# A batch's second-layer results kept in one PSUM bank, and added to x1 and the bias once per batch

## The chip, the cores and the metric

The kernel runs on one core of a Trainium2 chip. A time is the device time of one execution in microseconds (us). A core has five engines that each work through their own instructions strictly in order: TensorE (PE, with its weight loads PEld), VectorE (DVE), ScalarE (ACT), GpSimd (POOL) and SyncE (SP, which here only issues DMAs). They wait for each other by semaphores.

## What is computed

Input are 16 batches of 1024 nodes with 64 channels, `x`, and their adjacency matrices `adj` of zeros and ones. Two graph layers follow each other, each with a residual and a layer norm:

```python
x = _layernorm(x + _L0_gnn_ref(x, adj, nodemask, W1, b1, W2, b2))   # neighbours thinned out, weighted
                                                                    # quantiles of the rest, a small MLP
# second layer, h = x:
messages = jnp.einsum('bij,bjh->bih', adjacency, h)
node_in = jnp.concatenate([h, messages], axis=-1)
dh = jnp.tanh(node_in @ W1 + b1) @ W2 + b2
x = _layernorm(x + dh)
```

The change is in the second layer, at `... @ W2 + b2` and `x + dh`.

## The kernel before, in words

The batches are handled in groups (`GROUPS`, 2, 4, 4, 4 and 2 batches). Each group goes through three kinds of work, and those of different groups run beside each other.

- `prepare` (`list_batch`, L612, and `weigh_group`, L731) thins out the neighbours of each node and sorts the nodes by degree into lists in HBM.
- Chunks of tiles of 128 nodes: `fill` brings the neighbours' rows into slots (`slots_a`), by indirect DMAs on POOL (L846) or, in `ChunkByPE`, by one-hot matmuls on PE (`hot`, L982, and `p_slots`, L990). `select` (L862) sorts the slots with minima and maxima on DVE (L875), weights the chosen ones on ACT (`terms`, L897), sums them on PE (`p_g`, L894 and L899) and runs the MLP of the first layer: `p_h` (L903), `h_t` (L905), `p_y` (L908). DVE adds the bias (L910), the mask and the residual and does the layer norm (L550 to L558), and POOL scatters the rows to x1 in HBM (L916).
- `messages` (L1014) is the second layer of one batch. It loads the batch's x1 (`x_n` in the profile, L1018). For each of the batch's eight tiles (NT = 8, QT = 1) it then loads 128 rows of `adj` (L1024), transposes them on PE (`p_adj`, L1029) and copies them with ACT (`adj_t`, L1030), transposes x1's tile (`p_x`, L1035) and multiplies the adjacency with x1 (`p_msg`, L1039). ACT copies both into `node_t` (L1036, L1041). Then come the two layers of the MLP, `p_z` (L1043), `z_t` with tanh on ACT (L1045) and `p_d` (L1048). DVE adds the bias while it reads `p_d` from PSUM (L1049). After the eighth tile, DVE adds x1 (L1051) and does the layer norm, and SP stores the batch (L1053).

PSUM has eight banks. The pools give out the buffers of a tag in turn, in the order in which the code asks for them, and an instruction that writes a buffer waits until the last reader of its earlier use is done. The tags are "tr" and "ta" (one bank each), "rv" (three), "m" (two) and "y" (one). Tag "m" serves `p_g`, `p_h`, `p_x`, `p_msg`, `p_z` and two matmuls of `list_batch`. Tag "y" serves `p_y` and `p_d`.

The order of the work is set twice. The loop at the end (L1097 to L1141) calls the generators of the chunks (`fill`, `select`), of `prepare` for the next group and of `finish_group` (which calls `messages`) for the last group in turn, in shares. Then the scheduler of the tile framework places the instructions of all of them on the engines by its own estimate of when each will be ready. So the instructions of a `messages` tile stand between the sorting steps of a chunk on DVE, and between other matmuls on PE. Whatever stands behind a waiting instruction on the same engine waits too. After the last chunk only the `messages` of the last group are left. The code after L1158 is for other inputs; with these it does not run.

Of the kernel before, what the change touches and what calls it, by code (L numbers as in the profile page):

```python
# [9 lines left out]
F32 = mybir.dt.float32  # L10
# [10 lines left out]
P = 128  # L21
# [395 lines left out]
def kernel(  # L417
# [15 lines left out]
    nc = tc.nc  # L433
    B, N, C = x.shape
    H = w1a.shape[1]
    NT = N // P
    HALF = N // 2
    HT = NT // 2
    XCOL = N + 2 * INFO
    ROW = XCOL + 2 * C  # L440
    QT = 1
# [79 lines left out]
    def row_of(v, n, name):  # L521
        t = const.tile([P, n], F32, name=name)
        nc.sync.dma_start(t, bass.AP(tensor=v.tensor, offset=v.offset, ap=[[0, P], [1, n]]))
        return t
# [6 lines left out]
    def matrix_of(v, name):  # L531
        t = const.tile(list(v.shape), F32, name=name)
        nc.sync.dma_start(t, v)
        return t

    w1a_s, w2a_s = matrix_of(w1a, "w1a_s"), matrix_of(w2a, "w2a_s")
    w1b_s, w2b_s = matrix_of(w1b, "w1b_s"), matrix_of(w2b, "w2b_s")
    b1a_c, b1b_c = column_of(b1a, H, "b1a_c"), column_of(b1b, C, "b1b_c")
    b2a_r, b2b_r = row_of(b2a, C, "b2a_r"), row_of(b2b, C, "b2b_r")

    def bcast(v, n):
        return v[:, :, None].to_broadcast([v.shape[0], v.shape[1], n])
# [47 lines left out]
    ps_m = sort.enter_context(tc.tile_pool(name="ps_m", bufs=2, space=PSUM))  # L590
# [195 lines left out]
    class Chunk:  # L786
# [75 lines left out]
        def select(self):  # L862
            g, n, f = self.g, self.n, self.n * C
            bufs = (self.a.rearrange("p k t c -> p k (t c)"), self.b)
            x_s = self.x_s

            def view(buf, at, steps):
                v = bufs[buf][:, at]
                return bass.AP(tensor=v.tensor, offset=v.offset,
                               ap=[v.ap[0]] + [[s * f, c] for c, s in steps] + [[1, f]])  # L870

            for i, (op, rb, ra, side, ab, aa, bb, ba, dims) in enumerate(self.net["steps"]):
                if i % 4 == 3:
                    yield
                nc.vector.tensor_tensor(  # L875
                    view(rb, ra, [(d[0], d[1 + side]) for d in dims]),
                    view(ab, aa, [(d[0], d[1]) for d in dims]),
                    view(bb, ba, [(d[0], d[2]) for d in dims]),
                    op=ALU.min if op == "min" else ALU.max)
            yield  # L880
            y = work.tile([P, TMAX, C], F32, name="y")[:, :n]
            for h in range(0, n, HT):
                e = min(n, h + HT)
                cols = (e - h) * P
                g_t = work.tile([C, HALF], F32, name="g_t", tag="gh", bufs=1)
                p = ps_m.tile([P, 512], F32, name="p_g", tag="m")
                places = len(self.net["places"])
                for t2 in range(h, e, 2):
                    for first in range(0, places, 4):
                        count = min(4, places - first)  # L890
                        for t in range(t2, min(t2 + 2, e)):
                            col = slice((t - h) * P, (t - h + 1) * P)
                            if first == 0:
                                nc.tensor.matmul(p[:C, col], x_s[:, t], ident, start=t == h, stop=False)  # L894
                            terms = work.tile([P, 4, C], F32, name="terms")
                            for i, v in enumerate(self.chosen(t, first, count)):
                                nc.scalar.mul(terms[:, i], v,  # L897
                                              g.weight(self.t0 + t, first + i))
                                nc.tensor.matmul(p[:C, col], terms[:, i], ident, start=False,  # L899
                                                 stop=t == e - 1 and first + i == places - 1)  # L900
                nc.scalar.copy(g_t[:, :cols], p[:C, :cols])
                p = ps_m.tile([P, 512], F32, name="p_h", tag="m")
                nc.tensor.matmul(p[:H, :cols], w1a_s, g_t[:, :cols], start=True, stop=True)  # L903
                h_t = work.tile([H, HALF], F32, name="h_t", tag="gh", bufs=1)
                nc.scalar.activation(h_t[:, :cols], p[:H, :cols], AF.Relu, bias=b1a_c)  # L905
                p_y = ps_m.tile([P, HT, C], F32, name="p_y", tag="y", bufs=1)
                for t in range(h, e):
                    nc.tensor.matmul(p_y[:, t - h, :], h_t[:, (t - h) * P:(t - h + 1) * P], w2a_s,  # L908
                                     start=True, stop=True)
                nc.vector.tensor_add(y[:, h:e], p_y[:, :e - h],  # L910
                                     b2a_r[:, None, :].to_broadcast([P, e - h, C]))
            nc.vector.tensor_mul(y, y, bcast(g.mask[:, self.t0:self.t0 + n], C))
            nc.vector.tensor_add(y, y, x_s)
            layer_norm(work, y, y)
            for t in range(n):
                nc.gpsimd.indirect_dma_start(  # L916
                    out=g.x1, out_offset=bass.IndirectOffsetOnAxis(
                        ap=g.local[:, self.t0 + t:self.t0 + t + 1], axis=0),
                    in_=y[:, t, :], in_offset=None)
            yield  # L920
# [93 lines left out]
    def messages(g, b):  # L1014

        x1 = work.tile([P, NT, C], F32, name="x1_n", bufs=1)
        n0 = (b - g.b0) * N
        nc.sync.dma_start(x1, g.x1[n0:n0 + N, :].rearrange("(t p) c -> p t c", p=P))  # L1018
        d = work.tile([P, NT, C], F32, name="d", bufs=1)
        for h in range(NT // QT):  # L1020
            adj_t = nets.tile([P, NT, QUART], F32, name="adj_t", bufs=1)
            for t in range(QT):
                a = rows.tile([P, N], F32, name="a", bufs=3)
                nc.sync.dma_start(a, adj[b, (h * QT + t) * P:(h * QT + t + 1) * P, :])  # L1024
                for q in range(2):
                    p = ps_t.tile([P, HT, P], F32, name="p_adj", tag="ta")
                    for j in range(HT):
                        col = (q * HT + j) * P
                        nc.tensor.transpose(p[:, j, :], a[:, col:col + P], ident)  # L1029
                    nc.scalar.copy(adj_t[:, q * HT:(q + 1) * HT, t * P:(t + 1) * P], p)  # L1030
                yield
            node_t = work.tile([2 * C, QUART], F32, name="node_t", bufs=1)
            p = ps_m.tile([P, 512], F32, name="p_x", tag="m")
            for t in range(QT):
                nc.tensor.transpose(p[:C, t * P:(t + 1) * P], x1[:, h * QT + t, :], ident)  # L1035
            nc.scalar.copy(node_t[:C], p[:C, :QUART])  # L1036
            p = ps_m.tile([P, 512], F32, name="p_msg", tag="m")
            for j in range(NT):
                nc.tensor.matmul(p[C:2 * C, :QUART], x1[:, j, :], adj_t[:, j, :],  # L1039
                                 start=(j == 0), stop=(j == NT - 1))  # L1040
            nc.scalar.copy(node_t[C:], p[C:2 * C, :QUART])  # L1041
            p = ps_m.tile([P, 512], F32, name="p_z", tag="m")
            nc.tensor.matmul(p[:C, :QUART], w1b_s, node_t, start=True, stop=True)  # L1043
            z_t = work.tile([C, QUART], F32, name="z_t", bufs=1)
            nc.scalar.activation(z_t, p[:C, :QUART], AF.Tanh, bias=b1b_c)  # L1045
            p_d = ps_m.tile([P, QT, C], F32, name="p_d", tag="y", bufs=1)
            for t in range(QT):
                nc.tensor.matmul(p_d[:, t, :], z_t[:, t * P:(t + 1) * P], w2b_s, start=True, stop=True)  # L1048
            nc.vector.tensor_add(d[:, h * QT:(h + 1) * QT], p_d, b2b_r[:, None, :].to_broadcast([P, QT, C]))  # L1049
            yield  # L1050
        nc.vector.tensor_add(d, d, x1)  # L1051
        layer_norm(work, d, d)
        nc.sync.dma_start(out[b].rearrange("(t p) c -> p t c", p=P), d)  # L1053
        yield
# [6 lines left out]
    def finish_group(g):  # L1061
        for b in range(g.b0, g.b0 + g.count):
            yield from messages(g, b)
# [100 lines left out]
    ps_m = ctx.enter_context(tc.tile_pool(name="ps_m_g", bufs=2, space=PSUM))  # L1164
# [93 lines left out]
    with tc.tile_pool(name="dense", bufs=1) as dense, tc.If(general > 0), tc.For_i(0, B, 1) as b:  # L1258
# [18 lines left out]
        with tc.For_i(0, C, 1) as c:  # L1277
# [21 lines left out]
            for t in range(NT):  # L1299
                for h in range(2):  # L1300
# [3 lines left out]
                    for k in range(NT):  # L1304
                        nc.tensor.matmul(p[:, :HALF], val_t[:, k, t * P:(t + 1) * P],
                                         before[:, k, js].rearrange("p q j -> p (q j)"),
                                         start=(k == 0), stop=(k == NT - 1))
# [43 lines left out]
```

## Time and profile before

| what | value |
|---|---|
| median of six runs | 3864.01 us (3841.45 to 3886.79) |
| the profiled execution, its own time | 3870.59 us |
| its span, first to last instruction | 3868.9 us |
| mean granted TensorE clock | 0.804 |
| L1049, DVE, add of `p_d` and bias, x128 | 28.2 us busy, 220 ns each |
| L1051, DVE, add of x1, 128x512, x16 | 10.9 us busy, 682 ns each |
| L910, DVE, add of `p_y` and bias, x51 | 16.3 us busy, 320 ns each |
| L1048, PE, `p_d` | 128 matmuls in fp32, each shown as two rows |

In a line of a group, the columns are: line of the code, engine, operation, what it writes and reads, shapes, count; then busy time in us and the mean of one in ns; then the idle time of the engine just before these instructions, and what ended most of it. In a line of waits: who waited for whom, us in total, how often, the longest. In a timeline: start in us, duration, engine, line, operation, tiles, shapes, count, and in brackets the idle time before it with what ended it. "remote" is a semaphore whose giver the profile does not show, "issue" an idle time at whose end no semaphore is seen.

### The profile page before, as it was taken

The page shows a single profiled execution, that of the slowest core. Times are in us where ns is not written, and L with a number is a line of the kernel's source. Part 1 is how long each engine was busy: PE and PEld are TensorE (multiplying, and loading weights), DVE is VectorE, ACT ScalarE, POOL GpSimd, SP SyncE. Part 2 cuts the span into 40 slices and gives each one's busy share as a digit, 9 for nine tenths or more (in the row PEclk, how much of TensorE's full clock was granted, in tenths as well). Part 3 has the DMA queues.
Part 4 walks back from the last instruction along what each step waited for, and adds up shares of the span by engine and source line. Part 5 has one row for each costly group of instructions (what it writes and reads, how often), then busy time and mean ns, then how long its engine had stood idle before and what let it go on. Part 6 is the DMA issues. An engine that isn't in the chain of part 4 may idle for free. (4 is left out here: it accounts for less than half of the span.)

```text
span 3868.9 us, 65767 instructions
## 1 busy us (share of the span) xinstructions
PE 2587.8 (67%) x24920; PEld 1971.0 (51%) x25076; DVE 2392.8 (62%) x5580; ACT 1581.0 (41%) x4045; POOL 1489.1 (38%) x1512
## 2 busy tenths in 40 slices
PE   5545776465766587656877497646778376676687
PEld 2424554244654365535765375535567264565565
DVE  4546783564767477746877376746698376775461
ACT  6423456332443244533554254423355133343353
POOL 2253261443425523652453513552422543513310
PEclk8766888687877798778988698868789687788898
DMA  3401224131312222131333122212221121121222
GB/s 121 128 19 57 80 58 132 45 104 36 85 48 79 57 76 64 41 101 42 93 85 99 40 75 72 75 32 64 71 82 47 39 76 55 38 69 48 55 69 77
DMA packets 221333, 264.34 MB, mean 68 GB/s; under 512 B 147443, under 2 KB 148050, under 8 KB 221008
## 3 DMA queue, kind: packets, MB, share of 16 engines
q1 hardware_dynamic: 174288, 189.31, 17.1%
q0 software_dynamic: 46720, 70.74, 7.0%
q8 instruction: 199, 3.26, 0.4%
q14 instruction: 126, 1.03, 0.1%
HBM read 218.20 MB, written 46.40 MB: 68 GB/s over the span
## 5 line engine op out<-in xcount | busy, mean ns | idle before, releaser
L846 POOL DMA_INDIRECT slots_a<-in_x_dram,idx x1012 | 1148.4, 1135 | 956.2 <-issue 283.1
L990 PE MATMUL p_slots<-hot,parts 128*64 128x256 bf16 (+1 forms) x12288 | 824.8, 279 | 359.9 <-issue 303.7
L990 PEld LDWEIGHTS <-parts 128*64 128x64 bf16 x12288 | 669.2, 116 | 492.8 <-issue 466.0
L916 POOL DMA_INDIRECT x<-y,ids x128 | 172.7, 1349 | 934.3 <-DVE y L558 708.5
L982 DVE TENSOR_SCALAR hot<-val 128x2048 bf16<-128x2048 bf16 x456 | 305.8, 689 | 335.5 <-remote 271.0
L875 DVE TENSOR_TENSOR slots_b<-slots_a 128x256 f32<-128x256 f32 (+14 forms) x582 | 356.1, 627 | 158.1 <-PE p_chosen L1011 54.4
L1001 ACT COPY slots_a<-p_slots 128x512 f32<-128x512 f32 (+2 forms) x136 | 73.2, 538 | 730.4 <-PE p_slots L990 409.0
L899 PE MATMUL p_g<-ident,terms 128*64 128x128 f32 x1988 | 295.3, 304 | 66.8 <-ACT terms L897 52.2
L1039 PE MATMUL p_msg<-adj_t,x_n 128*64 128x128 f32 x2048 | 290.0, 294 | 48.3 <-issue 22.1
L899 PEld LDWEIGHTS p_g<-ident,terms 128*64 128x64 f32 x1988 | 252.4, 154 | 95.7 <-ACT terms L897 67.4
L875 DVE TENSOR_TENSOR slots_a<-slots_b 128x256 f32<-128x256 f32 (+11 forms) x526 | 285.9, 555 | 0.6
L1039 PEld LDWEIGHTS p_msg<-adj_t,x_n 128*64 128x64 f32 x2048 | 243.0, 147 | 81.0 <-issue 41.6
L660 PE MATMUL p_rank<-reach,nb_t 128*128 128x128 bf16 (+3 forms) x956 | 187.2, 332 | 122.2 <-ACT nb_t L654 79.0
L662 ACT ACTIVATE gone<-p_rank,s 128x512 bf16<-128x512 f32 x256 | 167.6, 684 | 170.4 <-remote 96.4
L1049 DVE TENSOR_TENSOR d<-p_d,b2b_r 128x64 f32<-128x64 f32 x128 | 28.2, 220 | 325.9 <-PE p_d L1048 220.0
L660 PEld LDWEIGHTS <-nb_t 128*128 128x128 bf16 x1024 | 100.6, 108 | 253.4 <-ACT nb_t L654 123.1
L1029 PE MATMUL p_adj<-ident,a 128*128 128x128 f32 x1024 | 193.4, 304 | 47.7 <-ACT adj_t L1030 31.0
L630 ACT ACTIVATE gone<-nb 128x512 bf16<-128x512 bf16 x256 | 159.8, 627 | 122.5 <-DVE nb L626 86.8
L825 DVE MAX8 key<-code 128x8 f16<-128x1024 f16 x170 | 207.3, 1219 | 2.0 <-DVE code L827 0.5
L712 POOL DMA_INDIRECT order<-nb,at_i x128 | 144.3, 1128 | 151.6 <-DVE at_i L708 59.6
L875 DVE TENSOR_TENSOR slots_b<-slots_b 128x256 f32<-128x256 f32 (+11 forms) x310 | 197.6, 637 | 0.4
L664 DVE TENSOR_SCALAR gone<-gone,s 128x1024 bf16<-128x1024 bf16 x128 | 62.5, 489 | 212.8 <-ACT gone L662 201.9
(189 smaller groups left out, 4719.4 us busy)
## 6 DMA issues: line engine op xcount, KB each, us to landing
a<-in_adj_dram SPq DMA_DIRECT2D x256, 512.0 KB
row_p<-order SPq DMA_DIRECT2D x64, 256.0 KB
slots_a<-in_x_dram,idx POOLq DMA_INDIRECT x1012
row<-order SPq DMA_DIRECT2D x192, 64.0 KB
nb<-in_x_dram SPq DMA_DIRECT2D x128, 32.0 KB
row<-order SPq DMA_DIRECT2D x32, 128.0 KB
x_s<-in_x_dram SPq DMA_DIRECT2D x16, 256.0 KB
x_n<-x SPq DMA_DIRECT2D x16, 256.0 KB
```

The source lines that it names most:

```text
L630: nc.scalar.activation(r[:, cols], nb[:, cols], AF.Copy, accum_out=m[:, h, t - half_b * HT:t - half_b * HT + 1])
L660: nc.tensor.matmul(p[:, c * P:], nb_t[:, (h * HT + c) * P:(h * HT + c + 1) * P], reach[:, :HALF - c * P], start=False, stop=c == HT - 1)
L662: nc.scalar.activation(r[:, h * HALF:(h + 1) * HALF], p, AF.Abs, bias=biases[h][:, col], scale=2.0)
L825: nc.vector.max(key[:, t, r:r + 8], code)
L846: nc.gpsimd.indirect_dma_start(out=self.a[:, at[k], t, :], out_offset=None, in_=x_rows, in_offset=bass.IndirectOffsetOnAxis(ap=idx[:, t, k ...
L875: nc.vector.tensor_tensor(view(rb, ra, [(d[0], d[1 + side]) for d in dims]), view(ab, aa, [(d[0], d[1]) for d in dims]), view(bb, ba, [(d[ ...
L899: nc.tensor.matmul(p[:C, col], terms[:, i], ident, start=False, stop=t == e - 1 and first + i == places - 1)
L916: nc.gpsimd.indirect_dma_start(out=g.x1, out_offset=bass.IndirectOffsetOnAxis(ap=g.local[:, self.t0 + t:self.t0 + t + 1], axis=0), in_=y[: ...
L982: nc.vector.tensor_scalar(hot[:, :, :, e], val, float(inside[at]), None, op0=ALU.is_equal)
L990: nc.tensor.matmul(p[i * C:(i + 1) * C, o:o + w], g.parts[2 * q + i][:, c, h], hot[:, c, i, :w], start=c == 0 and h == 0, stop=c == NT - 1 ...
L1029: nc.tensor.transpose(p[:, j, :], a[:, col:col + P], ident)
L1039: nc.tensor.matmul(p[C:2 * C, :QUART], x1[:, j, :], adj_t[:, j, :], start=(j == 0), stop=(j == NT - 1))
```

## The change

`p_d` becomes one tile of eight results (`NT` x 64 fp32, one whole bank), taken once per batch from tag "y", and each tile's matmul writes its own eighth. The eight adds of 64 columns (L1049) go. In their place there are two adds of 512 columns per batch: `d = x1 + bias` at the batch's start, and `d = d + p_d` after the eighth tile, in the place of `d = d + x1`. As `p_d` now holds "y" for a whole batch, `p_y` of the chunks moves to tag "m". In the changed file the lines of `messages` below L1019 stand two further down: the first new add is its L1020, `p_d` its L1049, the second new add its L1051; `p_x`, `p_msg` and `p_z` are at L1037, L1041 and L1045.

```diff
@@ select
-                p_y = ps_m.tile([P, HT, C], F32, name="p_y", tag="y", bufs=1)
+                p_y = ps_m.tile([P, HT, C], F32, name="p_y", tag="m")
                 for t in range(h, e):
                     nc.tensor.matmul(p_y[:, t - h, :], h_t[:, (t - h) * P:(t - h + 1) * P], w2a_s,
                                      start=True, stop=True)
@@ messages
         d = work.tile([P, NT, C], F32, name="d", bufs=1)
+        nc.vector.tensor_add(d, x1, b2b_r[:, None, :].to_broadcast([P, NT, C]))
+        p_d = ps_m.tile([P, NT, C], F32, name="p_d", tag="y", bufs=1)
         for h in range(NT // QT):
...
             nc.scalar.activation(z_t, p[:C, :QUART], AF.Tanh, bias=b1b_c)
-            p_d = ps_m.tile([P, QT, C], F32, name="p_d", tag="y", bufs=1)
             for t in range(QT):
-                nc.tensor.matmul(p_d[:, t, :], z_t[:, t * P:(t + 1) * P], w2b_s, start=True, stop=True)
-            nc.vector.tensor_add(d[:, h * QT:(h + 1) * QT], p_d, b2b_r[:, None, :].to_broadcast([P, QT, C]))
+                nc.tensor.matmul(p_d[:, h * QT + t, :], z_t[:, t * P:(t + 1) * P], w2b_s, start=True, stop=True)
             yield
-        nc.vector.tensor_add(d, d, x1)
+        nc.vector.tensor_add(d, d, p_d)
         layer_norm(work, d, d)
```

## The prediction

> **What bounds the kernel now.** I read the page's engine shares first, then the costliest groups, then the list of who waited for whom on VectorE, then the timeline of the longest wait, and last the timeline of the end.
>
> ```profile
> PE 2587.8 (67%) x24920; PEld 1971.0 (51%) x25076; DVE 2392.8 (62%) x5580; ACT 1581.0 (41%) x4045; POOL 1489.1 (38%) x1512
> ```
>
> No engine is full, so the kernel is bound by hand-overs between engines that each work strictly in order. The groups and the list of waits say where VectorE (DVE) stands still:
>
> ```profile
> L1049 DVE TENSOR_TENSOR d<-p_d,b2b_r 128x64 f32<-128x64 f32 x128 | 28.2, 220 | 325.9 <-PE p_d L1048 220.0
> ```
>
> ```profile
> DVE hot L982 <- remote: 271.0, 14, 71.6
> DVE d L1049 <- PE p_d L1048: 220.0, 59, 59.0
> DVE gone L664 <- ACT gone L662: 201.9, 47, 45.4
> DVE d L1049 <- remote: 71.3, 6, 31.5
> ```
>
> The add of L1049, which the change takes away, is the second costliest place at which DVE waits: 325.9 us of idle time for 28.2 us of work. Everything that comes later in DVE's order (sorting steps, `hot`, the layer norms) waits behind it. But a wait is worth only what would have run in it. The longest, on DVE and then on PE:
>
> ```profile
> 3021.57 1.23 DVE L825 MAX8 key<-code 128x8 f16<-128x1024 f16 x1
> 3081.82 0.23 DVE L1049 TENSOR_TENSOR d<-p_d,b2b_r 128x64 f32<-128x64 f32 x1 [59.03 <-PE p_d L1048]
> ```
>
> ```profile
> 3022.12 0.59 PE L672 MATMUL p_val<-nb,ident_h 128*128 128x512 bf16 x1 [2.04 <-ACT nb L677]
> 3058.26 0.69 PE L1043 MATMUL p_z<-node_t,w1b_s 128*64 128x128 f32 x2 [35.55 <-issue]
> 3080.76 0.68 PE L1048 MATMUL p_d<-w2b_s,z_t 64*128 64x64 f32 x2 [20.53 <-ACT z_t L1045]
> ```
>
> PE stands too, for 35.55 and 20.53 us: DVE is not what holds this stretch up, the PE-ACT chain in front of p_d is, and the change leaves that chain as it is. The last 94 us look the same in small:
>
> ```profile
> 3808.21 0.23 DVE L1049 TENSOR_TENSOR d<-p_d,b2b_r 128x64 f32<-128x64 f32 x1 [4.15 <-PE p_d L1048]
> ...
> 3812.58 0.23 DVE L1049 TENSOR_TENSOR d<-p_d,b2b_r 128x64 f32<-128x64 f32 x1 [4.15 <-PE p_d L1048]
> 3812.84 0.69 DVE L1051 TENSOR_TENSOR d<-d,x_n 128x512 f32<-128x512 f32 x1
> ...
> 3813.56 0.38 SPq L1018 DMA_DIRECT2D x_n<-x  x1
> ...
> 3817.37 0.42 PE L1035 MATMUL p_x<-ident,x_n 128*64 128x128 f32 x1 [2.77 <-DMA x_n<-x]
> ```
>
> One tile takes 4.4 us there, all of it PE and ACT, and DVE merely watches; the next batch's x1 is loaded only when L1051 has read the old one.
>
> **The change part by part.** The sum is made against the profiled execution, 3870.6 us (span 3868.9 and 1.7 around it), which is 6.6 us above the median of 3864.0.
>
> *Waits that go.* The 325.9 us of L1049 fall into 74.2 in the last 94 us, which hide behind PE and ACT (worth 0), and 251.7 before. Of these, 24 waits of 2 us or more make 218.9. After each I followed DVE in the timeline to its next stop. At 16 of them no engine waits for DVE before it stops again, 14 times within 6 us: late next is the result that DVE would have waited for anyway (an ACT square, a p_slots), so these are costed at nothing. Without that cover they would be worth up to the 251.7. At eight, another engine is seen waiting for DVE afterwards; counted as the smaller of the wait and of what the others then lose: at 1784 us 2.8, 2430 3.2, 2479 12.7, 2706 2.4, 3407 1.1, 3451 3.2, 3479 1.2, 3760 2.1. Together 28.7. The one at 2479 shows the mechanism: the layer norm of a chunk stands behind L1049, and POOL's scatter waits for it:
>
> ```profile
> 2479.41 0.23 DVE L1049 TENSOR_TENSOR d<-p_d,b2b_r 128x64 f32<-128x64 f32 x1 [16.72 <-PE p_nth L968]
> ...
> 2486.09 0.40 DVE L558 TENSOR_TENSOR y<-y,ln_st 128x256 f32<-128x256 f32 x1
> ```
>
> ```profile
> 2486.77 3.23 POOL L916 DMA_INDIRECT x<-y,ids  x1 [9.81 <-DVE y L558]
> ```
>
> Bounds 0 and 251.7; I take 28.7.
>
> *DVE work.* Out go 128 adds x 220 ns = 28.2 us and 16 of L1051 x 682 ns = 10.9. In come 16 of x1 + bias, shaped like L1051 (10.9), and 16 of d + p_d with 512 elements from PSUM, for which the trace has a row (L704 reads 128x512 from PSUM in 683 ns): 10.9. Net 17.3 us less. Bounds 0 and 17.3; DVE is busy 62% of the span and is late itself at some places and early at others, so neither end is nearer and I take the middle, 8.6.
>
> *The x1 load.* It no longer waits for L1051, only for the last p_msg and the early add, so on SP's queue it and the adj loads behind it leave earlier. In the last group, PE's p_msg before the boundary ends near 3810.4, and the load now starts at 3813.56: 3.2 us earlier. Elsewhere PE waits for x_n mostly at the first batch of a group (9.68 us at 3775, 10.97 at 3395), where the scatters on POOL decide, so only this boundary counts: 3.2. Adding d + p_d after the last tile costs what L1051 cost.
>
> *PE's waits on DVE, moved.* In the built program p_d waits on a DVE semaphore 77 times before and 7 after, p_y 21 and 0: before, both shared bank "y". That stall cost PE 10.1 us (p_d held by "DVE d L1049", 6.9 for the matmul and 3.2 for its weight load); p_y lost nothing to it. After, p_y takes a turn in the two-buffer ring "m", and whatever comes two turns later must wait for L910: p_msg waits on DVE 16 times (before 1), p_z 14 (0), p_x 5 (1), p_h 4 (1), 39 in all. Queued behind such a wait is all of PE: p_slots, p_rank, and ACT behind those. The trace doesn't have this wait. Below, it costs nothing, since L910 starts in the median 0.2 us after its p_y; above, all of L910's lags over the 51 adds, 36 us (the longest 5.1). I take 10, nearer to the median, since most tiles have a p_x before the p_msg that needs the buffer. So +10 and -10.1.
>
> Against this stands a rule. The Trainium skill's page "Perfetto Trace Analysis", section Optimizing Tensor Performance (Matmuls), wants independent matmul groups to rotate through different PSUM banks, so that one is evacuated while the next runs; putting p_y into a ring of two while p_d keeps a bank of its own for eight tiles goes the other way. By that rule the whole lag of 36 us would be exposed and the result be 26 us later, 3854; by the row of L910 it is mostly hidden. No run here shows it yet.
>
> *New waits on DVE.* 16 times the early add waits for the x_n load and for the previous batch's store of d (both on SP's queue). Below it costs less than nothing, as L1049 waited at the same places (13.31 us at 3782, 18.75 at 3403); above, five group starts x the 10.3 us that PE lost there (mean of 9.68 and 10.97), 52. I take 5, because the scheduler places the add near p_x, where DVE had stopped anyway.
>
> Sum: 3870.6 - 28.7 - 8.6 - 3.2 - 10.1 + 10 + 5 = 3835.0; less the 6.6 of this profile, **3828** on the scale of the medians.
>
> **The rivals.**
> 1. *The removed wait was the bound.* For it: 251.7 us of DVE standing in the middle, and the place at 2479. Against it: 16 of 24 waits end in another stop. If a third of the 251.7 comes through (84 in place of 28.7), 3773.
> 2. *A wait takes its place (slower).* The 39 PE waits behind L910. DVE's own stops are long (71.6 us at `hot`, 45.4 at `gone`); when L910 stands behind one, PE now stands too, and p_slots with it, which is what `hot` waits for. Against it: L910 lagged over 2 us at only six of 51. Slower than before from (36 + 10) / 39 = 1.2 us a wait, by over 1% from 2.2; at 2.5 us it costs 98 in place of 10: 3916.
> 3. *It does nothing that shows.* DVE stands just as long one instruction later (at `hot` or `ln_st`), new and old waits cancel, and only the boundary of 3.2 us is left: 3861. For it: the stretch at 3022 to 3080, in which PE stood too.
>
> **How the numbers follow.** Forecast 0.42, rival 1 0.17, rival 2 0.27, rival 3 0.14. The likeliest case by itself lies at 3795 to 3860 (lag cost 36 in place of 10; waits worth twice as much). Range 3750 to 3920: down to 107 of the 251.7 coming through, up to rival 2 at 2.6 us a wait; that leaves some 0.08 below and 0.12 above. One per cent, about what a measurement of this kernel can tell from no change (its six runs span 3841 to 3887), is 38.6 us. Faster by more (under 3825): rival 1 (0.17), nearly half of the forecast case (0.20), 0.01 of rival 3: 0.38. Slower by more (over 3903): 0.22 of rival 2, 0.04 from the others, by a new order of instructions that falls badly: 0.26. Between: 0.36.
>
> **What would show it.** After: 16 instructions of each new add, the second 0.68 us; no L1049-like group of 326 us idle; DVE's idle time before d + p_d near the 74 us of the end at most, since one add there waits for eight tiles. If `hot` and `ln_st` waits grow by over 150 us, rival 3 was right about where the idle time goes. PE's waits for "DVE y L910" at p_msg and p_z should sum to about 10 us; over 80 is rival 2. The x_n load at the last boundary should start about 3 us sooner after the last p_msg. The forecast fails above all if the unchanged PE-ACT stalls fall elsewhere, as a stretch like that at 3022 is alone 58 us.

## The result and the profile after

The changed kernel takes **3891.36 us** (median of 21 runs, 3867.75 to 3917.34), the kernel before 3859.17 us in the same runs (42 runs, 3836.73 to 3901.0). The ratio is 1.0079, with a 95% interval of 1.0059 to 1.0099: some 30 us slower, where 3828 and a gain of 0.9% had been forecast. The sign is wrong. Here and below, a ratio leaves out runs that took over 1.5% more than the fastest of the same kernel, so it is not exactly the ratio of two medians.

The page's engine shares of the changed kernel, and its span of 3878.4 us (before 3868.9):

```profile
span 3878.4 us, 65584 instructions
PE 2572.7 (66%) x24919; PEld 1950.1 (50%) x25076; DVE 2383.6 (61%) x5468; ACT 1578.0 (41%) x4041; POOL 1553.2 (40%) x1512
```

DVE is busy 9.2 us less than before, and the span is 9.5 us longer. So DVE stands 18.7 us more. Where it stands is in the costliest groups on DVE (the last part of a line is the idle time in front of the group):

```profile
L1051 DVE TENSOR_TENSOR d<-d,p_d 128x512 f32<-128x512 f32 x16 | 11.0, 685 | 83.5 <-PE p_d L1049 48.3 <-remote 34.8 <-PE p_nth L968 0.4
L1020 DVE TENSOR_TENSOR d<-x_n,b2b_r 128x512 f32<-128x512 f32 x16 | 10.9, 683 | 39.3 <-DMA x_n<-x 35.6 <-DMA out_dram<-d 3.6
L831 DVE TENSOR_TENSOR idx<-off,srt 128x48 int32<-128x48 f32 (+5 forms) x28 | 5.6, 199 | 69.0 <-DMA slots_a<-in_x_dram,idx 68.7 <-DVE off L830 0.2
```

The 325.9 us of idle time in front of the old add are gone. In their place stand 83.5 us in front of `d + p_d`, 39.3 in front of the new early add, and the rest in front of instructions that the edit does not touch: +68.6 us at L831, +38.5 at the sorting steps (L875, all its groups), +32.7 at L555, +24.0 at `hot`, +22.6 at L774, +21.9 at L1151 (in the end of the span, where it costs nothing) and +12.8 at L953. With the 325.9 taken off, these sum to +18.0 of the 18.7. The groups that are not listed (-15.9 at L772 and +10.6 at L623 are the largest) nearly cancel.

L831 is the surprise. Before, it had 0.4 us of idle time:

```profile
L831 DVE TENSOR_TENSOR idx<-off,srt 128x48 int32<-128x48 f32 (+5 forms) x28 | 5.6, 201 | 0.4 <-DVE off L830 0.2
```

It writes the list of indices (`idx`) for the gathers of a later chunk, into a buffer from which the gathers of an earlier chunk still read. The timeline of DVE in the changed kernel, where it comes to this instruction for the first of three long stops:

```profile
3284.35 0.41 DVE L875 TENSOR_TENSOR slots_b<-slots_a 128x256 f32<-128x256 f32 x1
3320.24 0.21 DVE L831 TENSOR_TENSOR idx<-off,srt 128x48 int32<-128x48 f32 x1 [35.48 <-DMA slots_a<-in_x_dram,idx]
3320.37 0.42 DVE L875 TENSOR_TENSOR slots_a<-slots_a 128x256 f32<-128x256 f32 x1
```

and on PE at the end of the same stop:

```profile
3320.84 0.47 PE L1011 MATMUL p_chosen<-ident,slots_a 128*128 128x128 f32 x1 [35.45 <-DVE slots_a L875]
```

DVE stands in the middle of a sort, whose next step starts 0.13 us after the instruction that held it, and PE waits for that sort. From 3285.39 to 3320.24 us, 34.9 us, neither PE nor ACT nor DVE does anything. The same instruction in the kernel before:

```profile
3321.82 0.36 DVE L875 TENSOR_TENSOR slots_a<-slots_a,slots_b 128x192 f32<-128x192 f32 x1
3322.22 0.21 DVE L831 TENSOR_TENSOR idx<-off,srt 128x48 int32<-128x48 f32 x1
```

It has no wait there, and it comes later in DVE's order: counted in the two traces, 2273 sorting steps stand in front of it before the change and 2248 after it. For the next chunk it is 2452 before and 2297 after (a stop of 25.31 us). Nothing in the diff concerns `fill`; the scheduler placed the instruction elsewhere when the adds around it changed.

The stop at L831 is not the whole of the loss, though. Both traces have the same 2799 sorting steps, in nearly the same order, and the start of the n-th shows roughly how far each kernel is. The 2000th starts 23.7 us later after the change than before, the 2200th 1.2 us, the 2500th 14.2 us. So some 13 us are lost where the two long stops at L831 lie; before that, the changed kernel had fallen behind by more and caught up again.

The second new place is a group's start. DVE (early add) and PE (`p_x`) wait together for x1, whose last rows POOL scatters (L916) among gathers that follow each other every 1.3 us:

```profile
1724.43 1.03 POOL L916 DMA_INDIRECT x<-y,ids  x1 [0.30 <-issue]
...
1726.66 0.38 SPq L1018 DMA_DIRECT2D x_n<-x  x1
...
1730.03 0.69 DVE L1020 TENSOR_TENSOR d<-x_n,b2b_r 128x512 f32<-128x512 f32 x1 [27.73 <-DMA x_n<-x]
...
1730.05 0.42 PE L1037 MATMUL p_x<-ident,x_n 128*64 128x128 f32 x1 [29.71 <-DMA x_n<-x]
```

I summed the stretches in which PE, PEld, ACT and DVE all stand: 638 us before, 674 after. Of those over 1 us, the ones that end at L831 went from 0 to 60.0, those that end with a load of x1 from 17.0 to 33.9, those that end with a late result ("remote") from 285.3 to 272.8, and those at whose end no semaphore is seen ("issue") from 168.1 to 134.4. So in this pair of profiles 77 us more are spent waiting for POOL's indirect DMAs, and some 41 less elsewhere.

### The profile page after: what moved, and what is told of

Its sections match the earlier page's. It is cut to its first block, busy times and chain, and to the rows that moved or that the text cites. A ratio compares the mean times of both kernels' runs of the same rounds, so it can differ in the third digit from the quotient of the medians.

```text
span 3878.4 us, 65584 instructions
## 1 busy us (share of the span) xinstructions
PE 2572.7 (66%) x24919; PEld 1950.1 (50%) x25076; DVE 2383.6 (61%) x5468; ACT 1578.0 (41%) x4041; POOL 1553.2 (40%) x1512
## 5 line engine op out<-in xcount | busy, mean ns | idle before, releaser
L846 POOL DMA_INDIRECT slots_a<-in_x_dram,idx x1012 | 1181.7, 1168 | 970.0 <-issue 287.2
L990 PE MATMUL p_slots<-hot,parts 128*64 128x256 bf16 (+1 forms) x12288 | 809.6, 277 | 266.0 <-issue 203.0
L990 PEld LDWEIGHTS <-parts 128*64 128x64 bf16 x12288 | 658.1, 116 | 395.2 <-issue 361.3
L916 POOL DMA_INDIRECT x<-y,ids x128 | 203.8, 1592 | 873.6 <-DVE y L558 588.8
L875 DVE TENSOR_TENSOR slots_b<-slots_a 128x256 f32<-128x256 f32 (+14 forms) x582 | 355.9, 627 | 195.9 <-remote 64.6
L1041 PE MATMUL p_msg<-adj_t,x_n 128*64 128x128 f32 x2048 | 289.2, 294 | 53.0 <-issue 42.3
L899 PEld LDWEIGHTS p_g<-ident,terms 128*64 128x64 f32 x1988 | 244.5, 151 | 114.5 <-ACT terms L897 86.9
L875 DVE TENSOR_TENSOR slots_a<-slots_b 128x256 f32<-128x256 f32 (+11 forms) x526 | 285.3, 555 | 0.6
L1041 PEld LDWEIGHTS p_msg<-adj_t,x_n 128*64 128x64 f32 x2048 | 242.4, 147 | 84.2 <-issue 59.2
L1031 PE MATMUL p_adj<-ident,a 128*128 128x128 f32 x1024 | 193.9, 303 | 38.5 <-issue 13.9
L712 POOL DMA_INDIRECT order<-nb,at_i x128 | 144.0, 1125 | 148.4 <-DVE at_i L708 61.1
L875 DVE TENSOR_TENSOR slots_b<-slots_b 128x256 f32<-128x256 f32 (+11 forms) x310 | 197.6, 637 | 0.5
L677 ACT ACTIVATE nb<-p_val 128x512 bf16<-128x512 f32 x256 | 151.7, 596 | 87.3 <-remote 52.0
```

Source lines behind the costliest of these rows:

```text
L846: nc.gpsimd.indirect_dma_start(out=self.a[:, at[k], t, :], out_offset=None, in_=x_rows, in_offset=bass.IndirectOffsetOnAxis(ap=idx[:, t, k ...
L875: nc.vector.tensor_tensor(view(rb, ra, [(d[0], d[1 + side]) for d in dims]), view(ab, aa, [(d[0], d[1]) for d in dims]), view(bb, ba, [(d[ ...
L916: nc.gpsimd.indirect_dma_start(out=g.x1, out_offset=bass.IndirectOffsetOnAxis(ap=g.local[:, self.t0 + t:self.t0 + t + 1], axis=0), in_=y[: ...
L990: nc.tensor.matmul(p[i * C:(i + 1) * C, o:o + w], g.parts[2 * q + i][:, c, h], hot[:, c, i, :w], start=c == 0 and h == 0, stop=c == NT - 1 ...
```

## The experiments

Theories, as the expectations name them: **A**, the early add of x1 + bias makes DVE wait for x1. **B**, `p_y` in the ring "m" makes PE wait for DVE. **C**, no term of the edit is to blame: it draws another order of the work, which meets POOL's gathers better or worse. In what follows a ratio is that to the kernel before on the same chip, with its 95% interval. "Late" results, of which the expectations speak, are told of in the last section.

### One part of the change alone

`py_in_m` is the kernel before with one line of the change:

```diff
-                p_y = ps_m.tile([P, HT, C], F32, name="p_y", tag="y", bufs=1)
+                p_y = ps_m.tile([P, HT, C], F32, name="p_y", tag="m")
```

> The kernel before with one edit: p_y takes its turn in tag m, everything else as before. The changed kernel took 1.0079 of the time before. Theory A (early add: the loss is DVE standing at the new add of x1 and bias until x1 has landed, 35.6 us in the trace after) expects 0.998 to 1.002 here, since there is no early add. Theory B (p_y in the ring of two makes PE wait for DVE) expects 1.005 to 1.010. Theory C (no step of the change costs anything itself; a new order of instructions meets the late hand-overs in the stretches of back-to-back gathers differently) expects any value from 0.99 to 1.01, unrelated to the waits on p_y, which stay under 10 us.

Measured: 1.0042 [1.0001, 1.0083].

`early_add` is the kernel before with the early add, the eight small adds then reading `d`, and no add of x1 at the end:

```diff
+        nc.vector.tensor_add(d, x1, b2b_r[:, None, :].to_broadcast([P, NT, C]))
...
-            nc.vector.tensor_add(d[:, h * QT:(h + 1) * QT], p_d, b2b_r[:, None, :].to_broadcast([P, QT, C]))
+            nc.vector.tensor_add(d[:, h * QT:(h + 1) * QT], d[:, h * QT:(h + 1) * QT], p_d)
...
-        nc.vector.tensor_add(d, d, x1)
```

> The kernel before with one edit: x1 and bias are added into d at the batch's start, each tile's add then adds p_d to its part of d, and the add of x1 at the end goes. p_y stays in tag y. Theory A (early add) expects 1.005 to 1.010, with 30 us or more of DVE idle time at the early add. Theory B (p_y in m) expects 0.998 to 1.002. Theory C (order) expects any value from 0.99 to 1.01.

Measured: 1.0004 [0.9970, 1.0038]. DVE stands 24.7 us in front of its early add.

`late_adds` is the changed kernel with both adds at the batch's end, so that nothing waits for x1 early:

```diff
-        nc.vector.tensor_add(d, x1, b2b_r[:, None, :].to_broadcast([P, NT, C]))
...
-        nc.vector.tensor_add(d, d, p_d)
+        nc.vector.tensor_add(d, x1, p_d)
+        nc.vector.tensor_add(d, d, b2b_r[:, None, :].to_broadcast([P, NT, C]))
```

> The changed kernel without its early add: after the eighth tile d = x1 + p_d and then d = d + bias, so 16 adds of 0.68 us (10.9 us of DVE) as before but at the end of the batch, and x1 is loaded after them as in the kernel before. p_y stays in tag m. Theory A (early add) expects 0.990 to 1.000. Theory B (p_y in m) expects 1.006 to 1.011. Theory C (order) expects any value from 0.99 to 1.01.

Measured: 0.9965 [0.9930, 1.0001]. Its DVE waits 54.0 us at L831 too, but the stretches there in which all engines stand sum to 4.9 us.

What follows: `early_add` does not bring the 0.8%. `py_in_m` comes out at half of it, with an interval that reaches the whole, though in the changed kernel's trace hardly any engine waits for L910. Who waited for that line, in the changed kernel:

```profile
who waited for it (us, times):
  PE p_h L903: 1.4, 1
  PEld p_msg L1041: 1.2, 2
  PE p_msg L1041: 0.7, 1
```

That is 2.1 us on PE: theory B has no wait to stand on. And `late_adds`, in which `p_y` is in "m" too, is not slower than the kernel before, where B expected 1.006 to 1.011. Taking the early add out gains 1.1%, which fits A, while putting it in alone costs nothing, which does not.

### Edits that should do nothing

`null_halves` splits the last add of the kernel before in two:

```diff
-        nc.vector.tensor_add(d, d, x1)
+        for e in range(2):
+            js = slice(e * HT, (e + 1) * HT)
+            nc.vector.tensor_add(d[:, js], d[:, js], x1[:, js])
```

> The kernel before, its last add of x1 split in two halves of 256 columns: 32 adds of 0.42 us in place of 16 of 0.68, which is 2.5 us more of DVE work and changes nothing else but the order in which the scheduler places the instructions. Theories A and B expect 0.999 to 1.001. Theory C (order) expects a value whose interval is clear of 1, between 0.99 and 1.01, in either direction, with the all-engine stops at other places.

Measured: 1.0026 [0.9985, 1.0066]. The interval is not clear of 1, as theory C expected it to be: this edit shows nothing either way.

`null_shares` changes in how many shares the loop at the end calls the chunks and `messages`; the instructions are the same, in another order:

```diff
-    SHARES = 24
+    SHARES = 25
```

> The kernel before with SHARES = 25 in place of 24: the generators take turns on a slightly different grid, every instruction stays. Theories A and B say nothing of it and expect 1.000. Theory C (order) expects a shift by up to 1% in either direction, with an interval clear of 1.

Measured: 1.0072 [1.0040, 1.0104]. An order that nobody designed costs as much as the change does. That is what C needs; but C allowed nearly any value within 1%, so it was hard to miss.

### The early add, at the fifth tile and in other orders

`mid_add` moves the line of the early add to the fifth tile, so that x1 would have long been there:

```diff
-        nc.vector.tensor_add(d, x1, b2b_r[:, None, :].to_broadcast([P, NT, C]))
...
+            if h == NT // QT // 2:
+                nc.vector.tensor_add(d, x1, b2b_r[:, None, :].to_broadcast([P, NT, C]))
```

> The changed kernel with the add of x1 and bias moved from the batch's start to its fifth tile, when x1 has long landed; everything else, p_y in m and the store behind it too, as in the changed kernel. Theory A (early add) expects 1.000 or less, that is 0.8% or more off the changed kernel, with no DVE idle time at that add. Theory B expects 1.006 to 1.010. Theory C expects any value from 0.99 to 1.01.

Measured: 0.9987 [0.9951, 1.0023]. But the scheduler left the add at the batch's start. In all 16 batches of `mid_add` it stands behind none to three of the batch's eight `p_x`, as in the changed kernel, in 13 of them behind the same number. At the group's start shown above, DVE and PE wait as before (the add is L1048 here):

```profile
1710.23 0.69 DVE L1048 TENSOR_TENSOR d<-x_n,b2b_r 128x512 f32<-128x512 f32 x1 [26.38 <-DMA x_n<-x]
1710.26 0.42 PE L1036 MATMUL p_x<-ident,x_n 128*64 128x128 f32 x1 [29.75 <-DMA x_n<-x]
```

DVE stands 35.5 us in front of the add in all, in the changed kernel 39.3. So `mid_add` is no test of theory A. It is the changed kernel in a slightly different order, and, on another chip, 0.9% away from it. The long waits for x1 need no early add: PE waits 26.8 and 22.5 us at two group starts in `null_shares`, which has no early add, and over 5 us at none but the last (9.6 us) in `early_add`, which has it.

`after_s25`, `late_s25`, `after_s23`, `late_s23`: the changed kernel and `late_adds` with SHARES 25 and 23.

> The changed kernel with SHARES = 25, which only shifts the turns of the generators; the kernel before with this edit took 1.0072 of the kernel before. Theory A (the early add at the batch's start costs about 1%, as the versions with the add in the middle or at the end, 0.9987 and 0.9965, seem to say) expects it at least 0.8% slower than late_s25 of this call. Theory C (order alone) expects the gap between the two to be anything from -1 to +1%.

> The changed kernel with both adds at the end of the batch (as in late_adds) and SHARES = 25. Theory A expects 0.8% or more below after_s25. Theory C expects any gap, and a value anywhere from 0.99 to 1.01, not near late_adds' 0.9965 by rule.

> The changed kernel with SHARES = 23. Theory A expects it at least 0.8% slower than late_s23 of this call; theory C expects the gap to be anything from -1 to +1%, so that over the three settings of SHARES the early add's sign changes or its mean comes near 0.

> The changed kernel with both adds at the end of the batch and SHARES = 23. Theory A expects 0.8% or more below after_s23. Theory C expects any gap.

Measured: 0.9994 [0.9961, 1.0027], 1.0034 [1.0005, 1.0064], 1.0105 [1.0062, 1.0147] and 0.9963 [0.9920, 1.0007].

`before_s23` and `mid_s23` fill the table (in `mid_s23`, too, the add stands behind none to three of the batch's `p_x`):

> The kernel before with SHARES 23 in place of 24: the same instructions, another order. If the change has a steady cost of its own (theory A or B), after_s23 (1.0105 of the kernel before) is over this run by about what after is over before, 0.8%: so this run gives near 1.003. If any edit only draws another order (theory C), it may give anything between 0.99 and 1.01, and the sign of after against before at this setting is open.

> The kernel after with the add of x1 + bias in front of the fifth tile's MLP, and SHARES 23. At SHARES 24 the move from the first to the fifth tile gave 0.9987 in place of 1.0079. If the early place of the add has a price in itself (theory A), this run is about 0.9% under after_s23: near 1.001. If the order decides (theory C), the difference can have either sign, within 1.5% of after_s23's 1.0105.

Measured: 1.0082 [1.0052, 1.0113] and 1.0146 [1.0107, 1.0184], on a chip that ran the kernel before in 3130.99 us (see the last section). Then the changed kernel and `late_adds` once more, with SHARES 24:

> The changed kernel once more, beside the same runs of the kernel before as the next one. On a chip that runs the kernel before in about 3860 us, with PE's results reaching ACT and DVE late during gathers, 1.008 again: order is fixed in the program, so what it draws is the same each time. On a chip like that of the last call (3131 us, no late hand-overs), theory C expects a gain nearer to that without gathers, 0.985 to 1.0; theory A expects 1.005 or more there too.

> The kernel after with both adds of 512 columns at the end of the batch, once more. At about 3860 us for the kernel before, 0.9965 again, so after over late 1.011. On a chip like that of the last call, theory A (the early add costs by waiting for x1) keeps the 1.011 between the two; theory C expects a ratio that need not be that, of either sign.

Measured: 1.0053 [1.0029, 1.0078] and 1.0100 [1.0068, 1.0132]; the kernel before took 3138.03 us there. The first is a miss for theory C, which expected 0.985 to 1.0 on such a chip, and within what A expected; the two together (0.995) are a miss for A.

| order | before | after | late adds | add written at the fifth tile |
|---|---|---|---|---|
| SHARES 24, chips at 3858 to 3872 us | 1 | 1.0079 | 0.9965 | 0.9987 |
| SHARES 25, chips at 3802 and 3858 us | 1.0072 | 0.9994 | 1.0034 | not run |
| SHARES 23, chip at 3802 us | not run | 1.0105 | 0.9963 | not run |
| SHARES 23, chip at 3131 us | 1.0082 | not run | not run | 1.0146 |
| SHARES 24, chip at 3138 us | 1 | 1.0053 | 1.0100 | not run |

What follows: theory A, a steady cost of the early add, falls. The early add against late adds is +1.1%, -0.4%, +1.4% and, on the last chip, -0.5% (the two medians, 3156.52 and 3172.68). `after_s25` stands 78.7 us in front of its early add, twice as long as the changed kernel with SHARES 24, and is the fastest of the three settings. The mean of the first three gaps is +0.7%, so a small price on average is not excluded. The change itself against the kernel before is +0.8% with SHARES 24 and -0.8% with 25 (0.9994 / 1.0072, each against the kernel before on its own chip). For SHARES 23 the two were run on chips of different kinds (1.0105 / 1.0082). No edit shows a sign of its own over these settings.

### Without gathers

`before_plain` and `after_plain` take POOL's gathers out: each slot's indirect DMAs are replaced by one plain load of the same size, of fixed rows (so the first layer's neighbours are not the right ones).

```diff
-                for t in range(n):
...
-                    nc.gpsimd.indirect_dma_start(
...
+                c = sum(k < cap for cap in caps)
+                nc.sync.dma_start(self.a[:, at[k], :c, :],
+                                  x_rows[:c * P, :].rearrange("(t p) c -> p t c", p=P))
```

> The kernel before, with each set of indirect gathers of one slot (L846 on POOL) replaced by one plain load of the same size and place on SP, of rows that do not depend on the graph; so the quantiles of these chunks are of other rows. POOL keeps its scatters (L712, L916). Theory C (hand-overs from PE come late while POOL gathers back to back, and these stops set the time) expects a fall by 300 us or more, to 0.92 or less, and the stops of all three compute engines, 638 us in the trace before, to fall under 250 us. If the stops are waits of the program's own (PE, ACT and DVE for each other), the time stays above 0.97.

> The changed kernel with the same replacement of the gathers as in before_plain. Set against before_plain of this call: Theory A (early add waits for x1) and theory B (p_y in m) expect it 0.5 to 1.5% slower than before_plain, as both waits need no gathers. Theory C expects it within 0.5% of before_plain or faster by up to 1%, as the prediction's terms said (fewer adds, fewer waits).

Measured: 0.7617 [0.7576, 0.7658] and 0.7559 [0.7521, 0.7597]. The page's engine shares of the one and of the other:

```profile
PE 2372.8 (81%) x24920; PEld 1881.7 (64%) x25076; DVE 2383.6 (81%) x5580; ACT 1575.4 (53%) x4045; POOL 438.5 (15%) x500
```

```profile
PE 2366.1 (81%) x24919; PEld 1870.5 (64%) x25076; DVE 2374.2 (81%) x5468; ACT 1571.3 (54%) x4041; POOL 525.0 (18%) x500
```

After over before is 0.7559 / 0.7617 = 0.992 (medians of five runs each, 2919.55 and 2942.21; 0.989 to 0.996 by the spread of these runs): the change gains 22.7 us. L831 has 0.1 us of idle time in both, and the stretches in which PE, PEld, ACT and DVE stand are 74 and 68 us long. Without waits for the gathers, the change has the sign of the prediction and two thirds of its 36 us. The terms are not measured one by one, and it is one pair of orders: no neutral edit was run without gathers, so how far another order moves the time there is not known.

### Pauses between the gathers

`spaced` is the kernel before, and `spaced_mid` is `mid_add`, with work on POOL behind each gather:

```diff
+                    for _ in range(8):
+                        nc.gpsimd.memset(pause, 0.0)
```

> The kernel before with eight memsets of 128x16 on POOL behind each gather of L846, into a tile that nothing reads: POOL works some 0.7 us between two gathers and is busy some 700 to 800 us longer. If the other engines' results come late because one gather follows the other without a pause, the stretches in which PE, ACT and DVE all stand shrink well below 638 us and the time falls or stays (0.90 to 1.00). If each gather delays them wherever it stands, or POOL's instructions of any kind do, the all-idle stretches stay at 600 us or grow and the time rises with the longer bursts, to 1.05 to 1.20.

> The kernel after with the add of x1 + bias in front of the fifth tile's MLP, and the same eight memsets behind each gather. If pauses help, this is the version to beat both kernels (below 0.99). If they do not, it lies within 1% of the run with the memsets in the kernel before, and shows what another order of the work is worth there.

Measured: 1.2982 [1.2938, 1.3027] and 1.3092 [1.3038, 1.3146]. The first lies outside both ranges expected, the second within 1% of the first. On what they were made for they are inconclusive: they ran on the chip with 3131 us, on which no result came late even without pauses. What they do show is the price of POOL's time. In the costliest groups on POOL in `spaced`, and in its list of waits:

```profile
L852 POOL MEMSET pause<- 128x16 f32 x8096 | 994.0, 123 | 460.6
```

```profile
DVE nb L626 <- DMA order<-nb,at_i: 900.5, 32, 148.5
```

The memsets took 994.0 us, with 460.6 between them, and the time rose by 934 us. In `before_s23` on the same chip the wait at L626 is 107.1 us. `prepare`'s scatters (L712) stand in POOL's queue behind the gathers, and all engines wait for them: the stretches in which all stand and that end with such a scatter sum to 844.9 us (54.8 in `before_s23`).

## Why the prediction was wrong

- **The failed step: the instructions that the edit does not touch were taken to stay in their places** ("the change leaves that chain as it is"). The sum has no term for a new order; it appears only as 0.04 of chance, for one "that falls badly". What the runs showed in its place: a new order alone moves the time by about as much as was forecast. The same instructions in another order took 1.0072 (`null_shares`) and 1.0082 (`before_s23`), and the change itself turns from +0.8% to -0.8% with SHARES 25. The forecast gain of 36 us (0.9%) lies within that. In this trace the move is seen at L831, 25 and 155 sorting steps earlier, which stops DVE for 35.5 and 25.3 us; stretches in which all engines stand and that end there went from 0 to 60.0 us. The prediction's own sign of failure, PE-ACT stalls that "fall elsewhere", is not what is seen: the stretches that end with a late result shrank by 12.5 us.
- **Where the gain went** is open. Without gathers the change gains 22.7 us. With gathers but without late results, on the chip at 3138 us, it costs 0.5% again, so late results are not needed for the loss. The waits at L831 are there again, 39.5, 25.3 and 25.7 us long (35.5, 25.3 and 7.9 in the first profile). From the list of waits of `after_again`:

```profile
DVE idx L831 <- DMA slots_a<-in_x_dram,idx: 90.4, 3, 39.5
DVE d L1020 <- DMA x_n<-x: 52.4, 4, 27.9
```

  All-engine stops that end at L831 or with a load of x1 sum to 128 us there, against 66 in `before_s23` (27.7 + 38.6). But `before_s23` takes as long (3155.91 us, `after_again` 3156.52, where the kernel before takes 3130.99 and 3138.03), so these stops do not tell the two apart; the kernel before with SHARES 24 was not profiled on such a chip. On the first chips it is the same: `late_adds` has 4.9 us of such stops at L831 and is the fastest, which fits, but `null_shares` and `after_s23` have none at L831 (48.1 and 57.9 with loads of x1) and cost 0.7% and 1.0%, and `mid_add` has 62.7 us of both kinds, against 17.0 in the kernel before, and costs nothing. That the waits for POOL's indirect DMAs, or L831's place, are the cause is therefore not shown. One more buffer for `idx` would test the latter; it wasn't tried.
- **Waits that go: 28.7 us forecast.** DVE's idle time did not fall at all (1472.6 to 1491.2 us). That fits the 16 waits costed at nothing, where another result was late next; the 28.7 can't be told apart in another order, and no run isolates them. The 83.5 us in front of `d + p_d` are somewhat over the 74 given as the most; 36.8 of them are in the end of the span.
- **DVE work: 17.3 us less forecast.** The adds came as costed (683 and 685 ns, in all 17.2 us less), but DVE's busy time fell by 9.2, as others took longer in the sum.
- **The x1 load at the last boundary: 3.2 us forecast.** Right. It starts at 3826.0 us, as the last `p_msg` of the batch ends (before: 3.2 us after it) and ahead of the add of 512 columns (3828.24), and PE no longer waits. From the last group's first `p_x` to the end of the span are 87.7 us, before 93.8.
- **PE's waits behind L910: 10 us forecast, 0 to 36 as bounds.** Measured 2.1 on PE and 1.2 on its weight loads, so the term was too large by some 7 us. Rival 2 named the right direction, but the wait that it named is not there. The 10.1 us of `p_d` behind the old add are gone, as forecast. The rule on PSUM banks in the Trainium skill's "Perfetto Trace Analysis" (Optimizing Tensor Performance (Matmuls)), from which the prediction drew that the whole 36 us would be exposed, did not decide here: in this ring of two 2.1 us were.
- **The early add: 5 us forecast, 52 as the upper bound.** DVE stands 39.3 us in front of it. What that costs is not shown; 27.7 of them are at the group's start where PE waits for the same load.
- **Rival 3** came nearest: the idle time came back elsewhere. Its test, `hot` and `ln_st` up by over 150 us, was not met (+24.0 and +43.0); the idle time came back at many places, most at one that the prediction didn't look at. And it expected nothing worse than no change.

The best orders seen, `late_adds` (0.9965) and `late_s23` (0.9963), beat both kernels by 0.4% on their chips with intervals that reach 1.000, and `late_adds` loses 1% on another. They are no version to keep for their edit.

## What to carry to other kernels

Where a scheduler places the work of several stages on engines that run in order, price an edit of a few tens of us against the spread of neutral edits, and run two of those first. Check in the trace that an experiment moved what it was to move: a line placed four tiles later in the code (`mid_add`) stayed at the same place on its engine. Before costing what is removed, list in the built order which untouched instructions moved, above all those that reuse a buffer still being read by a slow queue: here one address computation, 25 steps earlier, stopped DVE for 35.5 us. To see a stage's own gain, take the shared slow resource, here POOL's gathers, out of a pair of runs; a neutral edit belongs beside that pair too.

## What was not expected of the hardware

**Results that arrive late while POOL gathers.** In the first chips' traces, PE's results reach ACT and DVE up to tens of us late. ACT's timeline in the kernel before, in the stretch that the prediction shows:

```profile
3027.66 0.24 ACT L1036 COPY node_t<-p_x 64x128 f32<-64x128 f32 x1
3057.94 0.26 ACT L1041 COPY node_t<-p_msg 64x128 f32<-64x128 f32 x1 [30.04 <-remote]
3074.74 0.60 ACT L677 ACTIVATE nb<-p_val 128x512 bf16<-128x512 f32 x1 [16.54 <-remote]
```

and the matmul whose result L1041 copies, on PE's:

```profile
3016.93 0.64 PE L1039 MATMUL p_msg<-adj_t,x_n 128*64 128x128 f32 x4 [0.26 <-issue]
```

By the profile, which models the ends of matmuls, it ended at 3017.6; the copy began 40 us later, though ACT was free from 3027.9. So the trace does not tell whether PE finished late or its result was announced late. POOL issues gathers through that stretch, to 3076, each 1.00 us with 0.30 between them, and after that PE ends `p_d` at 3081.44 and DVE takes it 0.38 us later. ACT and DVE together wait 1131 us for such "remote" releases before the change, 1142 after it, and 51 without gathers. These waits overlap (the stretches in which all engines stand and that end so are 285 us before the change), so how much of what the gathers cost (0.7617 without them) is theirs is not shown. They are the "unchanged PE-ACT stalls" of the prediction. The Trainium skill's page "SBUF — State Buffer", section Who interferes with whom, says that PE and ACT never wait on anyone; it speaks of the memory's ports, and what delays these releases no run here shows.

**Two kinds of chip.** On the two chips that came last, the same kernel before took 3130.99 and 3138.03 us instead of 3802 to 3872, with a granted clock of 0.88 to 0.89 instead of about 0.81. There the "remote" waits of ACT and DVE are 0 to 2 us, and the gathers themselves are longer on average (the median is 1.05 us against 1.00, so the difference lies in some long ones). The group of the gathers in the kernel before, and in `before_s23`:

```profile
L846 POOL DMA_INDIRECT slots_a<-in_x_dram,idx x1012 | 1148.4, 1135 | 956.2 <-issue 283.1 <-ACT slots_a L840 181.2 <-PE p_adj L1029 71.5
```

```profile
L846 POOL DMA_INDIRECT slots_a<-in_x_dram,idx x1012 | 1374.0, 1358 | 695.5 <-issue 267.8 <-PE p_chosen L1011 69.3 <-ACT terms L897 62.7
```

1.36 us a gather, and no late results, against 1.14 us and late results. Why the chips differ is open; no chip was met both ways.
